# A gated expert network and a second network in one kernel: passes taken in sets, turned by block transposes and an exchange through DRAM

## The chip, the cores and the metric

The kernel runs on one core of one Trainium2 chip. The metric is the device time of one execution in microseconds; less is better. An engine here is TensorE (PE, and PEld for its weight loads), VectorE (DVE), ScalarE (ACT), GpSimd (POOL) or SyncE (SP, which only issues transfers).

## The reference, cut to what matters

```python
x = x + tanh(g_xattn) * experts(layernorm(x), token_ids, ctx)   # four experts, one for each token
x = x + tanh(g_ffn) * ffn(layernorm(x), w1, w3, w2, wr)

def experts(h, ids, W):            # Wg = Wu = Wd = ctx: one 512x512 matrix for each expert
    e = min(ids // 6250, 3)
    z = h @ W[e].T
    return (silu(z) * z) @ W[e].T

def ffn(h, w1, w3, w2, wr):        # 2048 tokens, width 512
    gates, idx = top_2(softmax(h @ wr.T))
    v = silu(silu(h @ w1.T) @ w3.T) @ w2.T
    out = zeros_like(h)
    out[idx[:, k]] += gates[:, k] * v    # only rows 0 to 7 are ever added to
```

There are 4 x 512 tokens of width 512, all in fp32. Only the first 8 rows of the output get anything from the second network, but every token contributes to them, so the second network runs over all tokens and is summed over them. The order in which it takes the tokens does not matter.

## The kernel before, in words

The kernel first sorts the tokens by expert. That gives 17 passes of 128 tokens each: 13 whole passes with one expert (0 to 12, `NF` is 13) and four split passes (13 to 16) in which each quarter of 32 tokens has its own expert. A short prelude on VectorE works out which token stands where (`from_row`, `to_row`) and which expert each pass has (`which`); TensorE runs filler matmuls (`busy`) meanwhile.

One pass goes through these steps, each a function of its own:

- `gather` (L389, POOL) fetches the pass's rows of x by an indirect DMA. `load` (L443, SP) fetches the expert's matrix, 1 MB, four for a split pass; a register load on SP finds the expert. The pool `mp` holds seven matrices.
- `centre` (L340 to L401, VectorE) takes the moments and subtracts the mean. `scale` and `norms` run `inverse_roots`, nine tiny VectorE instructions.
- `turn_in` (L380, TensorE; copy L410, ScalarE) turns the 128x512 tile by four 128x128 transposes through the identity, into PSUM (`tp_a`), and copies it to SBUF (`hT`).
- `up` (L453) multiplies by the matrix into `z`; ScalarE (L466) and VectorE (L467) form g = silu(z) z.
- `turn_mid` turns g in the same way (`tp_g`), `down` (L453) multiplies into `y`, VectorE (L481) adds to x, and POOL scatters the rows to the output (L482).
- `norms` normalizes the sum for the second network (L505), `turn_out` turns it (`tp_f`) and ScalarE copies it into `hT2`.

`z`, `y` and the second network's `v` and `Z` take turns in two PSUM buffers (`ps_mm`). A product of a whole pass is four fp32 matmuls of 128x512, each of which the profile shows as two.

The order of the work is written out by hand. `order` mixes split passes among the whole ones, and a loop runs over it: up of pass i, turn_in of i + 1, centre of i + 2, gather and load of i + 3, down of i - 1, turn_out of i - 2, and then `turn_mid` of i. So each matrix is loaded as its pass comes up, and each turn's copy lies beside a product.

The second network is a generator that `step` advances between those pieces. It takes two blocks of 1024 tokens (`b`). For each, `logits` (L699) gives the routing, `sums_of_hT` (L598 to L602) and `sums_of_w1` form the sums for a product with seven instead of eight parts (`X`, `Y`, `Z`, L622; `s1` holds the result), `route` picks the top two experts, and `second_layer` (L730 `v`, L742 `acc`) multiplies by w3 and sums over tokens. The end (`accT`, `out_product`, `ob`) finishes rows 0 to 7.

Of the kernel before, what the change touches and what calls it, by code (L numbers as in the profile page):

```python
# [17 lines left out]
ACT = mybir.EngineType.Activation  # L18

# [6 lines left out]
def tile_gated_moe_ffn(  # L26
# [58 lines left out]
    mp = ctx.enter_context(tc.tile_pool(name="mp", bufs=7))  # L85
    xp = ctx.enter_context(tc.tile_pool(name="xp", bufs=5))
    work = ctx.enter_context(tc.tile_pool(name="work", bufs=3))
    small = ctx.enter_context(tc.tile_pool(name="small", bufs=4))
    ps_mm = ctx.enter_context(tc.tile_pool(name="ps_mm", bufs=2, space=bass.MemoryType.PSUM))
# [23 lines left out]
    def load_w(src, name):  # L113
        w = ct_([P, KC, src.shape[1]], F32, name)
        nc.sync.dma_start(w, src.rearrange("(k p) f -> p k f", p=P))
        return w
# [25 lines left out]
    nc.vector.memset(steps, float(D))  # L142
    nc.vector.memset(steps[:, E - 1 : E], float(-(E - 1) * D))
# [100 lines left out]
    with nc.allow_low_precision("whole numbers below 4096"):  # L244
        nc.vector.tensor_reduce(which0, start, AX.X, ALU.add)
    nc.vector.tensor_mul(place, place, hot)
    padded = ct_([P, NJ], I16, "padded")
    with nc.allow_low_precision("whole numbers below 4096"):
        nc.vector.tensor_reduce(padded, place.rearrange("p e j -> p j e"), AX.X, ALU.add)
# [49 lines left out]
    with nc.allow_low_precision("whole numbers below 4096"):  # L299
        nc.vector.tensor_reduce(which, stepped.rearrange("p e n -> p n e"), AX.X, ALU.add)  # L300
# [4 lines left out]
    def row_tables():  # L305
# [18 lines left out]
            first, psum, float(-(NB - 1) * TB), float(TB), ALU.add, ALU.min  # L324
# [3 lines left out]
    hT2 = [ct_([P, KC, TB + (Q if b == NB - 1 else 0)], F32, f"hT2_{b}") for b in range(NB)]  # L328
# [9 lines left out]
    def moments(xt, name):  # L338
        st = small.tile([P, 6], F32, tag="st", name=f"st_{name}")
        nc.vector.bn_stats(st, xt)  # L340
        mv = small.tile([P, 2], F32, tag="mv", name=f"mv_{name}")
        nc.vector.bn_aggr(mv, st)
        return mv

    def inverse_roots(mvs_, names):
# [4 lines left out]
        def new(tag):  # L350
            return [small.tile([P, 1], F32, tag=tag, name=f"{tag}_{name}") for name in names]

        v, r, q, w, rs = new("v"), new("r"), new("q"), new("w"), new("rs")
        for i in n:
            nc.vector.tensor_scalar_add(v[i], mvs_[i][:, 1:2], EPS)
        for i in n:
            nc.vector.tensor_scalar(
                r[i].bitcast(I32), v[i].bitcast(I32), -0.5, float(0x5F3759DF), ALU.mult, ALU.add
            )
        for i in n:  # L360
            nc.vector.scalar_tensor_tensor(q[i], r[i], v[i], r[i], ALU.mult, ALU.mult)
        for i in n:
            nc.vector.tensor_scalar(w[i], q[i], 0.375, -1.25, ALU.mult, ALU.add)
        for i in n:
            nc.vector.tensor_scalar(w[i], w[i], q[i], 1.875, ALU.mult, ALU.add)
        for i in n:
            nc.vector.tensor_mul(r[i], r[i], w[i])
        for i in n:
            nc.vector.scalar_tensor_tensor(q[i], r[i], v[i], r[i], ALU.mult, ALU.mult)
        for i in n:  # L370
            nc.vector.tensor_scalar(q[i], q[i], -0.5, 1.5, ALU.mult, ALU.add)
# [11 lines left out]
    order = [0, 1, 2, 3, 4, 5, NF, 6, 7, 8, NF + 1, 9, 10, NF + 2, 11, 12, NF + 3]  # L383
    assert sorted(order) == list(range(NP))
    xs, x1s, mvs, rss, hs, hTs, gTs, gs, hs2, mats = {}, {}, {}, {}, {}, {}, {}, {}, {}, {}

    def gather(p):
        xt = xp.tile([P, D], F32, tag="x", name=f"x_{p}")
# [8 lines left out]
    def centre(p):  # L397

        mvs[p] = moments(xs[p], f"a{p}")
        hs[p] = work.tile([P, D], F32, tag="h", bufs=4, name=f"h_a{p}")  # L400
        nc.vector.tensor_scalar(hs[p], xs[p], mvs[p][:, 0:1], None, ALU.subtract)  # L401

    def scale(*ps):
        for p, rs in zip(ps, inverse_roots([mvs.pop(p) for p in ps], [f"a{p}" for p in ps])):
            rss[p] = rs

    def turn_in(p):
        tp = transposed(hs.pop(p), f"a{p}")
        hTs[p] = work.tile([P, KC * P], F32, tag="hT", bufs=2, name=f"hT_{p}")
        nc.scalar.copy(hTs[p], tp)  # L410

    def first_in(p):
# [5 lines left out]
        hTs[p] = work.tile([P, KC * P], F32, tag="hT", bufs=2, name=f"hT_{p}")  # L418
        n = D // 2
        for i in range(2):  # L420
# [7 lines left out]
            nc.scalar.copy(hTs[p][:, i * n : (i + 1) * n], tp)  # L428

    def load(p):  # L430

        n0, n = (p, 1) if p < NF else (NF + (p - NF) * G, G)
        mats[p] = []
        for i in range(n0, n0 + n):
# [4 lines left out]
                max_val=(E - 1) * D,  # L439
                skip_runtime_bounds_check_because="an expert's number, times D",  # L440
            )
            m = mp.tile([P, KC, D], F32, tag="m", name=f"m_{i}")
            nc.sync.dma_start(m, ctxT[bass.ds(at, D), :].rearrange("(k p) f -> p k f", p=P))  # L443
            mats[p].append(m)

    def expert_product(out_ps, lhs, p, inside=None):

        n = P // len(mats[p])
        for k in range(KC):
            if k == KC - 1 and inside is not None:  # L450
                inside()
            for i, m in enumerate(mats[p]):
                nc.tensor.matmul(  # L453
                    out_ps[i * n : (i + 1) * n, :],
                    lhs[:, k * P + i * n : k * P + (i + 1) * n],
                    m[:, k, :],
# [4 lines left out]
    def up(p, inside=None):  # L461
        z = ps_mm.tile([P, D], F32, tag="mm", name=f"z_{p}")
# [7 lines left out]
    def turn_mid(p):  # L470
# [3 lines left out]
        gTs[p] = gT  # L474

    def down(p):
        y = ps_mm.tile([P, D], F32, tag="mm", name=f"y_{p}")
        expert_product(y, gTs.pop(p), p)
# [12 lines left out]

    def norms(p_in, p_out):


        if p_out is None:
            return
        xt = x1s.pop(p_out)
        mv = [moments(xt, f"f{p_out}")]
        names = [f"f{p_out}"]
        if p_in is not None:  # L500
            mv.append(mvs.pop(p_in))
            names.append(f"a{p_in}")
        rs = inverse_roots(mv, names)
        h = work.tile([P, D], F32, tag="h", bufs=4, name=f"h_f{p_out}")
        nc.vector.tensor_scalar(h, xt, mv[0][:, 0:1], rs[0], ALU.subtract, ALU.mult)  # L505
# [4 lines left out]
    def turn_out(p):  # L510

        tp = transposed(hs2.pop(p), f"f{p}").rearrange("p (k t) -> p k t", k=KC)
        if p < NF:
            b, t = divmod(p, TB // P)
            nc.scalar.copy(hT2[b][:, :, t * P : (t + 1) * P], tp)  # L515
            return
        for i in range(G):
            n = (p - NF) * G + i
            place = NF * P + n * Q - (NB - 1) * TB
# [3 lines left out]
                min_val=min(place - E * (Q - 1), TB),  # L523
                max_val=min(place, TB),
                skip_runtime_bounds_check_because="its place less at most E (Q - 1) pads, at most TB",
            )
            nc.scalar.copy(hT2[NB - 1][:, :, bass.ds(at, Q)], tp[:, :, i * Q : (i + 1) * Q])

    def route(b, lt):
# [31 lines left out]
        nc.vector.tensor_sub(d, m1, m2)  # L561
        half = st("half", (P, TT))
# [10 lines left out]
        return g  # L573

    def sums_of_w1():

# [3 lines left out]
        ss = [ffp.tile([P, 2, h], F32, tag=f"S{i}", name=f"S{i}") for i in range(1, 5)]  # L580
# [10 lines left out]
    def sums_of_hT(b):  # L591


        lgs = [logits(b, half) for half in range(2)]
        b11, b12 = hT2[b][:, 0:2, 0:HB], hT2[b][:, 0:2, HB:TB]
        b21, b22 = hT2[b][:, 2:4, 0:HB], hT2[b][:, 2:4, HB:TB]
        ts = [ffp.tile([P, 2, HB], F32, tag=f"T{i}", name=f"T{i}_{b}") for i in range(1, 5)]
        nc.vector.tensor_sub(ts[0], b12, b11)  # L598
        lts[b] = [turned(b, half, lg) for half, lg in enumerate(lgs)]
        nc.vector.tensor_sub(ts[1], b22, ts[0])  # L600
        nc.vector.tensor_sub(ts[2], b22, b12)
        nc.vector.tensor_sub(ts[3], b21, ts[1])  # L602
        return b11, b21, b22, ts

    def first_layer(b):
# [14 lines left out]
        def product(out_ps, a, bb, c, start):  # L620
            for k in range(2):
                nc.tensor.matmul(  # L622
                    out_ps,
                    a[:, k, c * P : (c + 1) * P],
                    bb[:, k, :],
# [66 lines left out]
    def logits(b, half):  # L692
# [3 lines left out]
        for k in range(KC):  # L696
            cols = hT2[b][:, k, half * HB : (half + 1) * HB].rearrange("p (t c) -> p t c", t=TT)
# [14 lines left out]

    def ffn(b):

        yield from first_layer(b)
        for half in range(2):
            yield from second_layer(2 * b + half, route(2 * b + half, lts[b][half]))
# [3 lines left out]
    def second_layer(b, g):  # L721
# [3 lines left out]
        def gated(t, half=None):  # L725
# [3 lines left out]
            for k in range(KC):  # L729
                nc.tensor.matmul(  # L730
# [93 lines left out]
    SHORT = 1  # L824
    last = {b: max(i for i, p in enumerate(order) if min(p // (TB // P), NB - 1) == b) for b in range(NB)}
    running, hT_sums, lts, w1_sums = [], {}, {}, []

    def step():
        if running:
# [3 lines left out]
            if r in (0, SHORT):  # L833
                step()
# [3 lines left out]
    ffp = ctx.enter_context(tc.tile_pool(name="ffp", bufs=1))  # L838
    held = ct_([P, NU], I32, "held")

    def look_up(i):
        return which0[0:1, :] if i == order[0] else held[0:1, i : i + 1]

    load(order[0])
    gather(order[0])
    one = slice(order[1], order[1] + 1)
    nc.gpsimd.tensor_copy(held[0:1, one], which[0:1, one])
    load(order[1])  # L850
    for i in range(1, 5):
        gather(order[i])
    rest = slice(order[1] + 1, NU)
    nc.gpsimd.tensor_copy(held[0:1, rest], which[0:1, rest])
    first_in(order[0])
    scale(order[0])
    centre(order[1])
    scale(order[1])
    load(order[2])
    nc.sync.dma_start(gates[:, 0:1], g_xattn.to_broadcast([P, 1]))  # L860
    nc.sync.dma_start(gates[:, 1:2], g_ffn.to_broadcast([P, 1]))
    load(order[3])
    up(order[0], inside=lambda: turn_in(order[1]))
    centre(order[2])
    scale(order[2])
    up(order[1], inside=lambda: turn_mid(order[0]))
    turn_in(order[2])
    centre(order[3])
    nc.scalar.activation(tg, gates, AF.Tanh)
    down(order[0])  # L870
    turn_mid(order[1])
    norms(order[3], order[0])
    load(order[4])
    summing = sums_of_w1()
    owed = []
    for i in range(2, NP + 2):
        if i < NP:
            up(order[i])
        if i + 1 < NP:
            turn_in(order[i + 1])  # L880
        if i + 2 < NP:
            centre(order[i + 2])
        if i + 3 < NP:
            gather(order[i + 3])
            load(order[i + 3])
        if i <= NP:
            down(order[i - 1])
        turn_out(order[i - 2])
        if i <= NP:
            norms(order[i + 2] if i + 2 < NP else None, order[i - 1])  # L890
        step()
        if i > NP:
            step()
        if 5 <= i < 9:
# [68 lines left out]
```

## Time and profile before

| | |
|---|---|
| median of 3 runs | 277.63 us (277.48 to 277.67) |
| profiled execution | 277.53 us, its span 275.8 us |
| busy share of the span | PE 97%, PEld 45%, DVE 54%, ACT 25%, POOL 14% |
| moved by DMA | 42.54 MB; HBM read 38.10, written 4.47 |
| groups of products, busy | z 61.8, y 61.4, v 57.3 us |
| groups of turns, busy | tp_f 10.4, tp_g 10.2, tp_a 9.8 us |

A busy matmul in the profile overlaps the next one, so its mean duration (595 ns for 128x512) is longer than the distance between two. The chain of waits, followed back from the last instruction, gives each piece the time that it adds; that is the view to sum from. A group's row gives the line, engine, operation, tiles (out<-in), their shapes and the count, then the busy time and the mean of one in ns, then the idle time before it and what ended that. A line starting with a time gives start, length and what ran.

### The profile page before, as it was taken

How to read it: one execution, taken by the hardware profiler on the slowest of the kernel's cores; microseconds unless marked ns; L12 is line 12 of the kernel's file. 1: busy time of each engine (PE TensorE's matmuls, PEld its weight loads, DVE VectorE, ACT ScalarE, POOL GpSimd, SP SyncE). 2: the span in 40 equal slices, each digit the busy share in tenths (PEclk: the TensorE clock that was granted, in tenths of full speed). 3: DMA queues.
4: the chain of work that ended last, by engine and by line, in shares of the span. 5: the costliest groups of instructions: out<-in, count | busy, mean ns of one | idle time of the engine just before them, and what ended most of it. 6: DMA issues, size and time to landing. Idle time of an engine off the chain costs nothing.

```text
span 275.8 us, 3562 instructions
## 1 busy us (share of the span) xinstructions
PE 266.6 (97%) x1173; PEld 125.4 (45%) x1173; DVE 148.7 (54%) x593; ACT 69.3 (25%) x134; POOL 39.3 (14%) x63
## 2 busy tenths in 40 slices
PE   5889999999999999999999999999999999999994
PEld 2445455544355454444344444534245444344362
DVE  6677877777888769918263481516253620711000
ACT  2022232232232231223143232312113233311120
POOL 6520122221122211211110010101010000000000
PEclk9999999999999999999999999999999999999999
DMA  0697998545669996697304084001000000000000
GB/s 1 217 354 277 408 402 334 173 155 206 228 225 402 389 409 258 173 398 264 112 26 166 2 312 180 38 0 40 0 12 2 0 0 1 0 0 2 0 0 2
DMA packets 20722, 42.54 MB, mean 154 GB/s; under 512 B 2143, under 2 KB 2207, under 8 KB 20704
## 3 DMA queue, kind: packets, MB, share of 16 engines
q1 hardware_dynamic: 17952, 33.66, 34.0%
q0 software_dynamic: 2720, 8.65, 8.3%
q8 instruction: 9, 0.15, 0.2%
q14 instruction: 9, 0.07, 0.1%
q10 hardware_dynamic: 32, 0.01, 0.0%
HBM read 38.10 MB, written 4.47 MB: 154 GB/s over the span
## 4 chain that ended last, share of the span: by engine, by line
PE 94%; DVE 2%; DMA 2%; issue 1%; ACT 0%; DVEq 0%
PE z L453 22%; PE y L453 21%; PE v L730 20%; PE X L622 10%; PE Y L622 5%; PE tp_f L380 3%; PE tp_a L380 3%; PE tp_g L380 3%; PE Z L622 2%; PE acc L742 1%; PE lg L699 1%; DMA x<-in_x_dram,from_row 1%; DMA idt<-in_ids_dram 1%; PE accT L758 1%; PE o L814 0%
## 5 line engine op out<-in xcount | busy, mean ns | idle before, releaser
L453 PE MATMUL z<-m,hT 128*32 128x512 f32 (+1 forms) x232 | 61.8, 595 | 0.2 <-ACT hT L428 0.2
L453 PE MATMUL y<-m,gT 128*32 128x512 f32 (+1 forms) x232 | 61.4, 594 | 0.0
L730 PE MATMUL v<-w,s 128*128 128x512 f32 (+1 forms) x136 | 57.3, 570 | 0.0
L730 PEld LDWEIGHTS v<-w,s 128*128 128x128 f32 x136 | 25.0, 190 | 27.2 <-issue 26.7
L453 PEld LDWEIGHTS z<-m,hT 128*32 128x32 f32 (+1 forms) x232 | 22.6, 146 | 29.5 <-issue 28.1
L453 PEld LDWEIGHTS y<-m,gT 128*32 128x32 f32 (+1 forms) x232 | 22.6, 146 | 27.8 <-issue 27.8
L482 POOL DMA_INDIRECT out_dram<-x,to_row x17 | 17.2, 1011 | 84.9 <-DVE x L481 82.7
L389 POOL DMA_INDIRECT x<-in_x_dram,from_row x17 | 16.7, 984 | 77.5 <-DVE h_a L401 22.9
L467 DVE SCALAR_TENSOR_TENSOR g<-z,rs_a,g 128x512 f32<-128x512 f32 x17 | 12.7, 750 | 27.1 <-ACT g L466 27.0
L466 ACT ACTIVATE g<-z,rs_a 128x512 f32<-128x512 f32 x17 | 11.7, 687 | 51.3 <-PE z L453 51.3
L481 DVE SCALAR_TENSOR_TENSOR x<-y,tg,x 128x512 f32<-128x512 f32 x17 | 12.7, 749 | 16.9 <-PE y L453 16.8
L738 ACT ACTIVATE s<-v 128x512 f32<-128x512 f32 (+1 forms) x17 | 9.7, 572 | 41.9 <-PE v L730 41.9
L515 ACT COPY hT<-tp_f 128x512 f32<-128x512 f32 x13 | 7.6, 587 | 43.5 <-PE tp_f L380 43.5
L340 DVE BATCH_NORM_STATS2 st_a<-x 128x6 f32<-128x512 f32 x16 | 11.0, 688 | 7.5 <-DMA x<-in_x_dram,from_row 7.5
L622 PE MATMUL X<-T,S 128*128 128x512 f32 x32 | 15.0, 592 | 0.0
L380 PEld LDWEIGHTS tp_f<-ident,h_f 128*128 128x128 f32 x68 | 8.2, 141 | 10.2 <-issue 10.2
L340 DVE BATCH_NORM_STATS2 st_f<-x 128x6 f32<-128x512 f32 x17 | 11.8, 695 | 0.6
L380 PEld LDWEIGHTS tp_a<-ident,h_a 128*128 128x128 f32 x64 | 7.7, 140 | 9.4 <-issue 9.1
L640 DVE TENSOR_TENSOR s<-X,c 128x512 f32<-128x512 f32 x4 | 2.8, 692 | 16.2 <-PE X L622 16.2
L473 ACT COPY gT<-tp_g 128x512 f32<-128x512 f32 x17 | 10.0, 586 | 5.3 <-PE tp_g L380 5.3
L380 PE MATMUL tp_f<-ident,h_f 128*128 128x128 f32 x68 | 10.4, 276 | 0.0
L380 PE MATMUL tp_g<-ident,g 128*128 128x128 f32 x68 | 10.2, 273 | 0.0
(165 smaller groups left out, 271.6 us busy)
## 6 DMA issues: line engine op xcount, KB each, us to landing
m<-in_ctxT_dram SPq DMA_DIRECT2D x29, 1024.0 KB
w<-in_w1T_dram SPq DMA_DIRECT2D x1, 1024.0 KB
w<-in_w3T_dram SPq DMA_DIRECT2D x1, 1024.0 KB
w<-in_w2T_dram SPq DMA_DIRECT2D x1, 1024.0 KB
x<-in_x_dram,from_row POOLq DMA_INDIRECT x17, 6.2
out_dram<-x,to_row POOLq DMA_INDIRECT x17, 6.1
wr<-in_wrT_dram SPq DMA_DIRECT2D x1, 64.0 KB
x_first<-out_dram SPq DMA_DIRECT2D x4, 4.0 KB
```

The costliest lines, as they stand in the source:

```text
L340: nc.vector.bn_stats(st, xt)
L380: nc.tensor.transpose(tp[:, k * P : (k + 1) * P], h[:, k * P : (k + 1) * P], ident)
L389: nc.gpsimd.indirect_dma_start(out=xt, out_offset=None, in_=x, in_offset=bass.IndirectOffsetOnAxis(ap=from_row[:, p : p + 1], axis=0),)
L453: nc.tensor.matmul(out_ps[i * n : (i + 1) * n, :], lhs[:, k * P + i * n : k * P + (i + 1) * n], m[:, k, :], start=(k == 0), stop=(k == KC ...
L466: nc.scalar.activation(g, z, AF.Silu, scale=rs)
L467: nc.vector.scalar_tensor_tensor(g, z, rs, g, ALU.mult, ALU.mult)
L473: nc.scalar.copy(gT, tp)
L481: nc.vector.scalar_tensor_tensor(xt, y, tg[:, 0:1], xt, ALU.mult, ALU.add)
L482: nc.gpsimd.indirect_dma_start(out=out, out_offset=bass.IndirectOffsetOnAxis(ap=to_row[:, p : p + 1], axis=0), in_=xt, in_offset=None, bou ...
L622: nc.tensor.matmul(out_ps, a[:, k, c * P : (c + 1) * P], bb[:, k, :], start=start and k == 0, stop=k == 1, skip_group_check=True,)
L730: nc.tensor.matmul(v, s1[:, k, c_b + t * P : c_b + (t + 1) * P], w3[:, k, c0 : c0 + n], start=(k == 0), stop=(k == KC - 1),)
L738: nc.scalar.activation(s2, v, AF.Silu)
```

## The change

Four things are changed together.

First, the matrices of the four experts stay in SBUF (`cts`), loaded once by `load_cts` after the loads of passes 0, 1 and 2. From pass 3 on, `find` reads the expert's offset into a register of TensorE and the matmul's moving operand is addressed by it. Of the split passes, 13 and 15 load into `mp` (now four buffers) and 14 and 16 over `cts`.

Second, passes 4 to 11 are taken in sets. All of their up products are done before their down products. Their tiles are not turned by TensorE: VectorE's block transpose turns 32x32 blocks into a pair's buffer (inside `s1`, two passes interleaved, so the elements of one pass stand 8 apart), and `exchange` moves the blocks between partitions, four writes to DRAM and one read back, all on SP. The same is done for g, and, in sets of four passes, for the normalized sums of passes 0 to 11 (`turn_f`, `exchange_f`, three sets).

Third, `centre`'s subtraction and the normalization of passes 0 to 11 are done by ScalarE (`AF.Identity` with bias and scale), and the inverse roots of several passes by one batch.

Fourth, the order is written out anew. Pass 12 comes among the first whole passes, the split passes come last, and the second network's first block begins after pass 13. `far` holds the rows of passes 4 to 11, and later the sums T.

```diff
-    mp = ctx.enter_context(tc.tile_pool(name="mp", bufs=7))
+    mp = ctx.enter_context(tc.tile_pool(name="mp", bufs=4))
...
+    cts = ct_([P, E * KC * D], F32, "cts")
+
+    def load_cts(e):
+        nc.sync.dma_start(
+            cts[:, e * KC * D : (e + 1) * KC * D].rearrange("p (k f) -> p k f", k=KC),
+            ctxT[e * D : (e + 1) * D, :].rearrange("(k p) f -> p k f", p=P),
+        )
...
-        nc.vector.tensor_scalar(hs[p], xs[p], mvs[p][:, 0:1], None, ALU.subtract)
...
+        nc.scalar.activation(hs[p], xs[p], AF.Identity, bias=mvs[p][:, 0:1], scale=-1.0)
...
+            if p < NF or (p - NF) % 2 == 0:
+                m = mp.tile([P, KC, D], F32, tag="m", name=f"m_{i}")
+            else:
+                j = (i - n0) * KC * D
+                m = cts[:, j : j + KC * D].rearrange("p (k d) -> p k d", k=KC)
...
+    def find(p):
+
+        at = nc.values_load(
+            which[0:1, p : p + 1],
+            engines=[PE],
...
+        mats[p] = [lambda k: cts[:, bass.ds(at + k * D, D)]]
...
     def up(p, inside=None):
+        if 3 <= p < NF:
+            find(p)
...
+    def exchange(flat, name):
+
+        copy = dram.tile([P, 4, flat.shape[2]], F32, tag=name, name=name)
+        for q in range(4):
+            nc.sync.dma_start(
+                copy[q * Q : (q + 1) * Q].rearrange("f g c -> g f c"), flat[:, q, :]
+            )
+        nc.sync.dma_start(flat, copy)
...
+    pairs = {
+        j: s1.rearrange("p k t -> p (k t)")[:, (j - 2) * KC * 2 * P : (j - 1) * KC * 2 * P]
+        .rearrange("p (g t i k) -> p g t i k", g=4, i=2, k=KC)
+        for j in range(2, NS // 2)
+    }
+
+    def pair_part(p, h):
+        j, i = divmod(p, 2)
+        nc.vector.transpose(
+            pairs[j].rearrange("p q t i k -> p k q t i")[:, :, :, :, i],
+            h.rearrange("p (k q t) -> p k q t", k=KC, q=4),
+        )
...
+    def pair_columns(p):
+        j, i = divmod(p, 2)
+        part = pairs[j].rearrange("p g t i k -> p i k (g t)")[:, i]
+        return lambda k, c0, c1: part[:, k, c0:c1]
...
+    def norm_f(p):
+        rs, shift = scaled.pop(p)
+        h = work.tile([P, D], F32, tag="h", bufs=4, name=f"h_f{p}")
+        nc.scalar.activation(h, x1s.pop(p), AF.Identity, bias=shift, scale=rs)
+        hs2[p] = h
+
+    def turn_f(p):
+        b, i = divmod(p, 4)
+        nc.vector.transpose(
+            hT2[b].rearrange("p q k (i t) -> p k q i t", i=4)[:, :, :, i, :],
+            hs2.pop(p).rearrange("p (k q t) -> p k q t", k=KC, q=4),
+        )
...
+    load(2)
     nc.sync.dma_start(gates[:, 0:1], g_xattn.to_broadcast([P, 1]))
     nc.sync.dma_start(gates[:, 1:2], g_ffn.to_broadcast([P, 1]))
...
+    gather(4)
+    gather(5)
+    nc.gpsimd.memset(cts[0:1, 0:1], 0.0)
+    for e in range(E):
+        load_cts(e)
+    gather(6)
+    gather(7)
+    gather(12)
...
+    centre(12)
+    up(3)
+    scale(12)
+    down(2, inside=lambda: (turn_mid(3), turn_in(12)))
+    centre(8)
+    up(12)
+    turn_a(8)
+    centre(9)
+    down(3)
+    turn_a(9)
+    exchange_pair(4, "a")
+    scale_some(4, 4)
+    up(4, inside=lambda: turn_mid(12))
+    centre(10)
+    turn_g(4)
+    turn_a(10)
+    centre(11)
+    down(12)
+    turn_a(11)
+    exchange_pair(5, "a")
+    up(5)
+    turn_g(5)
+    exchange_pair(2, "g")
+    stats_f(0)
+    stats_f(1)
+    up(6)
...
+    exchange_pair(5, "g")
+    load(NF, 2, 4)
+    exchange_f(0)
+    for p in range(4, 8):
+        down(p)
+        stats_f(p)
+        next(summing)
...
+    roots_f(1)
+    down(8)
+    norms_turned(4, 4)
+    exchange_f(1)
+    stats_f(8)
+    down(9)
+    stats_f(9)
+    turn_in(NF)
+    centre(NF + 1)
+    down(10)
+    stats_f(10)
+    up(NF)
+    down(11, inside=lambda: turn_mid(NF))
+    load(NF + 1)
+    stats_f(11)
+    roots_f(2)
+    norm_f(8)
+    norm_f(9)
+    down(NF)
+    sums = sums_of_hT(0)
+    next(sums)
+    next(sums)
+    running.append(ffn(0))
+    norms(NF + 1, NF)
...
+    for p in range(8, 12):
+        turn_f(p)
+    exchange_f(2)
+    load_w(w3T, w3)
```

`turn_a(p)` and `turn_g(p)` are `pair_part` of the centred rows and of g, and `exchange_pair(j, ...)` is `exchange` of pair j, that is passes 2j and 2j + 1. `stats_f` takes the moments of a sum, `roots_f(b)` the inverse roots of four passes, `scale_some` those of several inputs. `sums_of_hT` is now a generator: logits of one half, logits of the other half with the first two sums T, and then one more sum at each step.

## The prediction

> **What bounds the kernel now.** I read the chain of waits first, then the same chain in order of time, the groups by shape, and the DMA rate in 2 us windows. The chain's shares by engine and line, and eight of its pieces:
>
> ```profile
> PE 94%; DVE 2%; DMA 2%; issue 1%; ACT 0%; DVEq 0%
> PE z L453 22%; PE y L453 21%; PE v L730 20%; PE X L622 10%; PE Y L622 5%; PE tp_f L380 3%; PE tp_a L380 3%; PE tp_g L380 3%; PE Z L622 2%; PE acc L742 1%; PE lg L699 1%; DMA x<-in_x_dram,from_row 1%; DMA idt<-in_ids_dram 1%; PE accT L758 1%; PE o L814 0%
> ```
> ```profile
> 27.89 3.44 PE z L453 x8
> 31.32 0.44 PE tp_a L380 x4
> 31.76 3.44 PE y L453 x8
> 35.20 0.44 PE tp_f L380 x4
> 35.63 0.44 PE tp_g L380 x4
> 36.07 3.43 PE z L453 x8
> ```
>
> Each piece starts where the one before ends: from the first z at 15.44 us TensorE is never waiting. So the time is the sum of TensorE's pieces: 3.44 us for a whole product, 0.44 us for one turn (four transposes through the identity). Whatever leaves TensorE is gained, as long as nothing else becomes late. The other engines have room on the mean, VectorE 54% and ScalarE 25% of the span; the DMA engines have none at 26 to 40 us:
>
> ```profile
> 22.00:24.00 2.00, 2.00 (x12) 1.35 (x11) 1.76 (x9) 0.97 (x2) 0.00 (x0) 1.00 0.40 133
> 28.00:30.00 2.00, 2.00 (x6) 0.88 (x5) 1.90 (x10) 0.51 (x1) 1.02 (x1) 1.00 1.05 409
> ```
>
> The last two columns are the DMA share and GB/s: 409 GB/s is the ceiling. The dip at 22 to 24 is the two loads of `gates`, 128 elements of 4 bytes each, third in the queue's order behind three matrices.
>
> Four rows price what the trace does not show directly (a strided read on VectorE, a block transpose, a strided and a plain weight load), and one answer shows the register loads:
>
> ```profile
> L300 DVE TENSOR_REDUCE which<-stepped 128x29 int32<-128x203 f32 x1 | 0.5, 525 | 0.0
> L710 DVE STREAM_TRANSPOSE lt<-lg 128x128 f32<-128x128 f32 x4 | 1.1, 303 | 2.2 <-PE lg L699 2.2
> L276 PEld LDWEIGHTS <-atlane 128*128 128x128 f16 x16 | 1.0, 152 | 1.2 <-DVE atlane L258 0.8 <-issue 0.5
> L200 PEld LDWEIGHTS <-ones 128*128 128x128 bf16 x31 | 3.3, 112 | 4.3 <-issue 1.9
> ```
> ```profile
> L520 ACTq TENSOR_LOAD <-first x16: 274/276/477, 81.8 to 208.8; - x16
> ```
>
> **What the Trainium skill says.** VectorE: DVE Perf Modes, "The three transpose paths": VectorE turns 32x32 blocks only, so blocks must still change partitions; that is what the DRAM exchange is for. `lt` in the trace is used in exactly such blocks. DMA: Bandwidth & Descriptors, "Two DMAs through the same engine are not ordered": a DMA that reads what another wrote must be issued after the first one's completion; so each exchange is two legs in series, with SP held between them. Before has no such pair. SBUF — State Buffer, "Door 1: The DMA port swizzle": steps of more than four fp32 pay per access. The trace agrees for VectorE reads and weight loads (below). No run here shows a strided write.
>
> **The change, part by part.**
>
> *Turns off TensorE.* Passes 4 to 11 lose tp_a and tp_g, passes 0 to 11 lose tp_f: 8 + 8 + 12 = 28 turns x 0.44 = **-12.3 us**. Products, logits and the second network keep their TensorE instructions. The weight loads from exchanged pairs step 8 elements. Strided against plain costs 152 against 112 ns for 16-bit; the same ratio puts the 190 ns of fp32 at 260, and a matmul lasts 430. Cost 0 behind the matmul before; without that cover, 128 loads x the excess over 430.
>
> *VectorE and ScalarE.* Sixteen `centre` (486 ns) and twelve norm (542 ns) passes leave VectorE for ScalarE, at about 0.65 us each (629 for a ScalarE SBUF pass, L647), and ScalarE loses 28 copies of 0.59: +18.2 - 16.5, nothing. VectorE gets 28 block transposes. From 303 ns for 128 elements over a floor of 155 (the one-element rows), 512 cost about 0.75 us. The 16 of inputs and g write with a step of 8; the strided reduce above costs (525 - 155) / 203 = 1.8 ns an element, so 155 + 512 x 1.8 = 1.08 us. Bounds 0.75 and 2.2; I take 1.1 for these, 0.75 for the 12 of f, whose runs are 32 long. The walk from up(4) to up(11), 31.4 us on TensorE: 8 g (0.75), 8 turn_g (1.1), 4 x 0.87 stats_f, bn of 10 and 11 1.7, turn_a 2.2, y12 0.75, two batches of roots 5.0, 4 turn_f 3.0: 31 us. VectorE is full there. Pass 12's norms then hold y of pass 4 until about 92, where its product ends at 87.6; its PSUM buffer is wanted by down(6) at 91.2: 1.5 us late, and 1.0 later at up(13). At 0.75 a transpose nothing is late. Taken: **+1.3** (0 to 2.5).
>
> *The four resident matrices.* up(3) waits for all of them. In the chain it would start at 35.9 (36.07, less a tp_f, plus a late gT copy on ScalarE behind two `centre`, +0.25). By 14 us the windows add up to 1.56 MB moved. Still to come: the rest of seven matrices at 1.05 MB, nine gathers at 0.26, one scatter and half of two more gathers: 10.35 - 1.56 = 8.8 MB at 409 GB/s = 21.5 us, plus about 2 for the `gates` dip (windows 18 to 26 lack 1.15 MB, some of which gathers can fill), plus 0.5 to land: 38.0 to 38.3. **+2.4** (0 to 5): the matrices that trickled in one per pass are now due at once. Their issue waits for a memset on POOL behind gathers 4 and 5 (1.26 us apart), at about 17; exchange a2, w1 and all later loads stand behind them on SP, none wanted before 52.
>
> *Register loads on TensorE.* Nine `find`, each a load and register arithmetic. On ScalarE's queue a load took 276 ns and, behind a waiting copy, ran only when that copy started; the copies then follow each other 0.43 apart instead of 0.27. If TensorE's sequencer runs ahead it costs 0, if not 0.3 each: **+0.9** (0 to 2.7).
>
> *Exchanges.* Eleven on SP, four of a, four of g, three of f: 14.7 MB more, against 6 MB of matrices less. Price of a leg, from the idt load (1.74 us for next to nothing): 1.7 + bytes / 409 GB/s; so 3.0 for a pair, 4.3 for f. a2: issued behind the matrices, back at 45, wanted by up(4) at 52.7. g: the last is issued at 88 and back by 97, wanted by down(10) at 106. f1 is the tight one: down(7) ends at 98.3 to 100, then stats, roots (2.5), norms and four transposes to 108 to 110, two legs 8.6: back at 117 to 119, wanted by the second logits at 121 to 123. Behind it on SP wait the loads of pass 14 (they wait for down(11) anyway, at 117; 10.2 us of data, landed 131; wanted 133.9). Cost **0**; cover 2 to 7 us. The price from the other side, the 6.1 us median of a gather of 0.26 MB, gives a leg of 8.1 and is a rival below. Scatters and gathers on POOL keep their number; the last ones only free buffers.
>
> *Order at the ends.* X after the logits waits for T and `lt` on VectorE (L598 1.22 + 0.3 after y's 0.75): **+0.55**. The last lg now comes 1.4 us after tp_f and waits for a Silu and four copies on ScalarE, 2.5: **+1.1**, before it lay 10 us later. Two late copies, at up(12) and the second y: **+0.2**; the late gT: **+0.25**.
>
> Sum: -12.3 + 1.3 + 2.4 + 0.9 + 0 + 0.55 + 1.1 + 0.45 = **-5.6 us**. The profiled execution took 277.53 (span 275.8 and 1.7 around it), 0.1 from the median of the runs; so **271.9**. A measurement here tells 0.2% (0.55 us) from no change.
>
> **Rivals.**
>
> *Everything hides*: transposes at 0.75, matrices in time, registers free. 277.5 - 12.3 + 1.1 + 0.55 = 266.3, at the very best 265.2. For it: each stall has zero within its bounds. Against: the strided read's 1.8 ns, and 409 GB/s is a hard ceiling.
>
> *Late transfers*: a leg costs 8.1 us for 1 MB. f1 is back at 126 where 122.8 is wanted, +3.4: 275.3. For it: 6.1 us for a quarter MB. Against: that is from POOL, with its descriptor work of 1 us and a busy queue.
>
> *Slower: VectorE becomes the bound.* Ten strided transposes lie between up(4) and down(4). From 1.1 us on each further 0.1 us is 1.0 us of lag, and TensorE follows two PSUM buffers behind. It decides from 1.65 us a transpose, where the 5.6 are eaten; at 2.2, the upper bound, 271.9 + 11 = 283. For it: no strided write is in the trace. Against: strided reads cost 1.75 times, not 3 times.
>
> *The change does not do what it says*: the split passes still load 16 matrices, so DMA only falls from 29 to 23; if the matrices were what bounds, little would change. The chain says they do not.
>
> **The numbers.** Forecast 0.56 (269 to 275), everything hides 0.22, late transfers 0.11, VectorE-bound 0.11. 271.9 is the likeliest. Range 265.5 to 279: the forecast, nearly all of the first rival, the second, and the mildest of the third. Faster: 0.55 + 0.22 + 0.08 = 0.85; same 0.03; slower 0.12.
>
> **What would show it.** Right: no tp of passes 4 to 11, tp_a, tp_g and tp_f groups of 32, 36 and 20 transposes; z waiting for DMA once, 2 to 3 us, near 36; strided transposes near 1.1 us; VectorE over nine tenths at 53 to 90; weight loads under 300 ns. Wrong: X or lg waiting for DMA near 120; weight loads above 430; a gap of 0.3 us at each find; z waiting for exchanged pairs. A total under 266 would mean that the stalls hide, over 277.5 that one of the last two rivals holds.

## The result, and the profile after

The changed kernel takes **334.06 us** (median of 4 runs, 332.51 to 335.16) where the kernel before, on the same chip, takes 277.62 (277.48 to 277.67): a ratio of 1.203, 95% interval 1.198 to 1.208. The forecast was 271.9, at most 279.0. It was wrong in sign and by 62 us. Where the executions of one kernel below fall into two groups some per cent apart, its time and ratio are those of the faster group; only the profile of the kernel with one load behind each of four exchanges is of the slower one.

The page of the profile after: the span, the busy time of TensorE, and three of the rows of 40 slices (8.3 us each).

```profile
span 330.7 us, 3331 instructions
...
PE 273.9 (83%) x1061; PEld 132.6 (40%) x1061; DVE 144.4 (44%) x464; ACT 74.0 (22%) x134; POOL 38.9 (12%) x64
...
PE   5999379999979409788106999959999999999995
PEclk9999869999979957979656999999999999999999
DMA  0889953643347663844439627997400000000000
```

TensorE, which never waited before from its first product on, now has holes at slices 5, 14 and 15, 20 to 22 and 27. The clock row falls to 5 to 7 at and behind most of them. At 5 and 27 the DMA row shows 9, loads that fill the engines; in the longest hole, 20 and 21, it shows 4 and 3: there the DMA engines are far from full. The waits say for what (engine, line, what was waited for, us in total, times, longest):

```profile
PE lg L843 <- DMA hT<-f: 19.5, 2, 16.5
PE y L514 <- DMA s<-g: 15.1, 2, 12.7
PE z L514 <- DMA cts<-in_ctxT_dram: 7.1, 1, 7.1
PE z L514 <- DMA m<-in_ctxT_dram: 6.8, 4, 1.8
```

35 us of waits are for what exchanges brought back (`hT<-f`, `s<-g`), 7.1 for the resident matrices at up(3), 6.8 for loads of split passes. The chain, which was 94% TensorE before, can be followed back to 188 us only; the second fence is a piece of it in order of time:

```profile
PE 35%; DMA 5%; ACTq 1%; ACT 1%; issue 0%; DVE 0%
```
```profile
202.24 2.45 PE X L766 x6
204.69 14.90 DMA m<-in_ctxT_dram
```

Those loads of pass 15 could not be issued before 201.7, when SP was done with f2. SP's own waits and its instructions between 132 and 172 us show what held it (start, length, queue, line, what, how many):

```profile
SPq L567 <- DMA f<-hT: 37.7, 7, 9.1
SPq L567 <- DMA g<-s: 29.1, 8, 7.2
SPq L567 <- DMA a<-s: 28.6, 6, 9.2
```
```profile
132.19 8.46 SPq L564 DMA_DIRECT2D f<-hT  x4
153.02 0.35 SPq L567 DMA_DIRECT2D hT<-f  x1
153.47 2.92 SPq L564 DMA_DIRECT2D f<-hT  x4
171.03 0.35 SPq L567 DMA_DIRECT2D hT<-f  x1
```

L564 is the write leg, L567 the read leg. f1's write begins at 153.47 and is read at 171.03: 17.6 us for a leg that I had at 4.3. f0's, behind two loads of matrices, took 20.8. The first 5 us of f1's write go beside f0's read of 1 MB, with a DMA share of 0.70 to 0.97 from 155 to 158 us; then the engines empty. No engine computes from 162 to 176; the windows within f1's write there give the DMA share and GB/s in the last two columns:

```profile
166.00:167.00 1.00, 0.00 (x0) 0.00 (x0) 0.00 (x0) 0.00 (x0) 0.00 (x0) 0.50 0.25 96
168.00:169.00 1.00, 0.00 (x0) 0.00 (x0) 0.00 (x0) 0.00 (x0) 0.00 (x0) 0.50 0.26 100
```

A share of 0.25 at 100 GB/s fits four of sixteen engines busy all the time. The target of each write is `copy[...].rearrange("f g c -> g f c")`: its outermost dimension is the four groups g. The Trainium skill, DMA: Bandwidth & Descriptors, "Why a DMA increments its semaphore by 16 and not by 1", says under "How many engines (k)" that a DMA takes "the largest k ≤ 16 that divides both of those dim sizes", the slowest dimensions of its two sides. I had read the page for another of its sections. That is the theory that the experiments test first; the rivals are that short runs or DRAM writes are slow in themselves, and that SP's order does the harm.

### The profile page after: what moved, and what is told of

Its sections match the earlier page's. It is cut to its first block, busy times and chain, and to the rows that moved or that the text cites. A ratio compares the mean times of both kernels' runs of the same rounds, so it can differ in the third digit from the quotient of the medians.

```text
span 330.7 us, 3331 instructions
## 1 busy us (share of the span) xinstructions
PE 273.9 (83%) x1061; PEld 132.6 (40%) x1061; DVE 144.4 (44%) x464; ACT 74.0 (22%) x134; POOL 38.9 (12%) x64
## 5 line engine op out<-in xcount | busy, mean ns | idle before, releaser
L514 PE MATMUL y<-cts,s 128*128 x64 | 33.6, 675 | 15.2 <-DMA s<-g 15.1
L514 PEld LDWEIGHTS y<-cts,s 128*128 128x128 f32 x64 | 19.7, 319 | 27.4 <-issue 19.6
L514 PE MATMUL z<-m,hT 128*32 128x512 f32 (+1 forms) x88 | 24.6, 668 | 7.0 <-DMA m<-in_ctxT_dram 6.8
L514 PE MATMUL z<-cts,s 128*128 x64 | 28.5, 598 | 0.1
L514 PEld LDWEIGHTS z<-cts,s 128*128 128x128 f32 x64 | 19.9, 314 | 8.0 <-DVE g L530 1.0
L514 PE MATMUL z<-cts,hT 128*32 128x512 f32 (+1 forms) x80 | 16.2, 618 | 7.1 <-DMA cts<-in_ctxT_dram 7.1
L529 ACT ACTIVATE g<-z,rs_a 128x512 f32<-128x512 f32 x17 | 11.7, 686 | 46.1 <-PE z L514 42.0
L514 PE MATMUL y<-m,gT 128*32 128x512 f32 (+1 forms) x88 | 18.3, 596 | 0.0
L766 PE MATMUL X<-far,S 128*128 128x512 f32 x32 | 15.1, 595 | 0.6 <-ACT u L777 0.6
L514 PEld LDWEIGHTS z<-m,hT 128*32 128x32 f32 (+1 forms) x88 | 6.9, 143 | 21.6 <-DMA m<-in_ctxT_dram 10.9
L544 DVE SCALAR_TENSOR_TENSOR far<-y,tg,far 128x512 f32<-128x512 f32 x8 | 6.0, 745 | 21.5 <-PE y L514 21.5
L766 PE MATMUL Y<-far,w 128*128 128x512 f32 x32 | 15.2, 592 | 0.0
```

The lines of the kernel that those rows point to most:

```text
L514: nc.tensor.matmul(out_ps[i * n : (i + 1) * n, :], lhs(k, i * n, (i + 1) * n), m(k), start=(k == 0), stop=(k == KC - 1),)
L529: nc.scalar.activation(g, z, AF.Silu, scale=rs)
L544: nc.vector.scalar_tensor_tensor(xt, y, tg[:, 0:1], xt, ALU.mult, ALU.add)
L766: nc.tensor.matmul(out_ps, a[:, k, c * P : (c + 1) * P], bb[:, k], start=start and k == 0, stop=k == 1, skip_group_check=True,)
```

## The experiments

Ratios are to the kernel before, run beside it on the same chip, with 95% intervals. Exchanges are named by what they carry and by pair or set: a4 is the a of passes 8 and 9, f1 the f of passes 4 to 7.

### Writes by source group

```
-        for q in range(4):
-            nc.sync.dma_start(copy[q * Q : (q + 1) * Q].rearrange("f g c -> g f c"), flat[:, q, :])
+        for g in range(4):
+            nc.sync.dma_start(
+                copy[:, g, :].rearrange("(q f) c -> f q c", q=4), flat[g * Q : (g + 1) * Q])
         nc.sync.dma_start(flat, copy)
```

> The same bytes go to the same places in the same runs of 1 and 2 KB by four DMAs, but each DMA now takes the 32 partitions of one source group (outermost dimension 32 on both sides) instead of all 128 partitions with the target's four groups outermost. Theory (the outermost 4 confines each write to 4 of the 16 DMA engines): DMA share during writes rises from 0.26 towards 1, the SP wait between write and read falls from 7 to 9 us to 2 to 3, logits and down products wait for exchanges 0 to 3 us in all instead of 35, and the whole lands at 268 to 276 us, 272 the likeliest. Rival (short runs or DRAM writes themselves are slow, about 100 GB/s): no change, 330 to 336 us. Second rival (SP in order is what hurts, with loads behind exchanges): legs hardly shorter, total above 310 us.

289.07 us, ratio 1.036 (1.029 to 1.042); span 287.7 against 330.7. Four lines and the same bytes gave back **43 us** of span. f1's write now leads to its read in 8.9 us instead of 17.6, the pair a3 in 5.5 instead of 9.1. But the time is 13 us above the upper end of this run's forecast. Two waits of size stay; the forecast had given 0 to 3 us to all waits for exchanges:

```profile
123.25 2.55 SPq L564 DMA_DIRECT2D f<-hT  x4
132.14 0.34 SPq L567 DMA_DIRECT2D hT<-f  x1
```
```profile
PE lg L843 <- DMA hT<-f: 7.0, 1, 7.0
PE z L514 <- DMA cts<-in_ctxT_dram: 4.5, 1, 4.5
```

### The permutation in the read leg

```
-        for g in range(4): ...
-        nc.sync.dma_start(flat, copy)
+        nc.sync.dma_start(copy, flat)
+        for q in range(4):
+            nc.sync.dma_start(
+                flat[q * Q : (q + 1) * Q], copy[:, q, :].rearrange("(g f) c -> f g c", g=4))
```

> One plain write of 128 partitions with runs of 4 or 8 KB, then four reads, each into 32 partitions, in runs of 1 or 2 KB: the permutation is made by the read leg, and all five DMAs have an outermost dimension of 32 or 128. Theory (number of engines): as fast as the version that writes by source group, within 2 us of it, 268 to 276 us. Rival (short runs into DRAM are slow, reads are not): clearly faster than the version that writes short runs, by 20 us or more, since here only the read has short runs.

294.07 us, 1.053 (1.046 to 1.059): 40 us better than the change as well, though 5 us behind the version before it, not within 2. Long runs into DRAM are no better than short ones: that rival falls. Here one DMA writes a pair, and where nothing stands ahead (a4, a5) its write leads to the reads in 3.1 and 3.0 us, which is the price that the prediction had. Why the whole is 5 us slower was not followed up; it waits 8.9 us for f1 and 2.7 for a pair of g.

### Two engines

```
         for q in range(4):
+            for g in (0, 2):
                 nc.sync.dma_start(
-                    copy[q * Q : (q + 1) * Q].rearrange("f g c -> g f c"), flat[:, q, :])
+                    copy[q * Q : (q + 1) * Q, g : g + 2].rearrange("f g c -> g f c"),
+                    flat[g * Q : (g + 2) * Q, q, :])
```

> The changed kernel with each write cut in two, so that the outermost dimension of each of the eight DMAs is 2 instead of 4; same bytes, same runs, same places. Theory (the outermost dimension sets the number of DMA engines): the DMA share during an f write falls from 0.26 to 0.13 and the rate from about 100 to about 50 GB/s, a pair's write takes 11 to 14 us, and the total is 370 to 420 us. Rival (the order of rows or the short runs set the rate): the rate stays at 80 to 100 GB/s and the total within 330 to 350 us, the four more issues of 0.5 us each included.

404.99 us (one run). Windows during f1's write, which now takes 25.6 us up to its read:

```profile
218.00:222.00 4.00, 0.00 (x0) 0.00 (x0) 0.00 (x0) 0.00 (x0) 0.00 (x0) 0.50 0.13 51
```

Outermost dimension 4: share 0.25, 100 GB/s. Outermost dimension 2: share 0.13, 51 GB/s. Half the share, half the rate: some 25 GB/s for each of four or two engines, and 409 / 16 is 25.6. So runs of 1 and 2 KB cost no rate here. This settles it between the two readings: with the same bytes, runs and places, the rate follows the outermost dimension. (A pair took 14.4 to 14.9 us where 11 to 14 were forecast.)

### Order alone, with the narrow writes

The changed kernel with an own matrix for pass 3 and early loads of pass 13 (both edits are shown below), and its own writes.

> The changed kernel with its writes confined as they were (outermost dimension 4), but with the two repairs of order: an own matrix for pass 3 and the early loads of pass 13. If order on SP was the main fault, this alone comes near the version with both, under 285 us. If the four engines of the writes are the main fault, the legs stay at 7 to 9 us for a pair and 13 or more for f, SP is still occupied by them, and the total stays above 300 us; 312 is my estimate.

336.38 us (one run), no better than the change at all, and 24 above the estimate for it. These two changes of order gain nothing while the writes are narrow; they are not what made the 43 us.

### No exchange

```
     def exchange(flat, name):
+        return
```

> Leaves out all eleven exchanges, writes and reads, so products and logits of passes 0 to 11 read blocks that have not changed partitions; every other instruction stays. Theory (the exchanges alone make the loss): 267 to 273 us, the sum of my prediction without them, with up(3) waiting 2 to 4 us for the resident matrices and no other wait of TensorE above 1.5 us. Rival (resident matrices, the register loads or VectorE make a large part): above 280 us, with waits of TensorE for those. The difference to the kernel with wide writes is what eleven exchanges cost when they use all DMA engines; I expect 0 to 4 us.

278.35 us, ratio 0.995 (0.993 to 0.998); span 276.9. The theory had said 267 to 273, so at least 5 us of loss lie outside the exchanges. And eleven exchanges on all engines cost 10.8 us of span (287.7 - 276.9), where 0 to 4 were forecast. Apart from the start (2.9 us, in every kernel here), the waits have one entry of size:

```profile
PE z L514 <- DMA cts<-in_ctxT_dram: 5.6, 1, 5.6
```

The product behind it took 5.59 us instead of 3.4 to 3.7, in a stretch (35 to 50 us) with a mean clock of 0.77: 7.6 us in all at a place where I had put 2.4.

### An own matrix for pass 3

On the version that writes by source group:

```
     nc.sync.dma_start(gates[:, 1:2], g_ffn.to_broadcast([P, 1]))
+    load(3)
...
-        if 3 <= p < NF:
+        if 4 <= p < NF:
             find(p)
```

> On the version that writes by source group: pass 3 loads its own matrix into the fourth buffer ahead of the four resident ones, which are then first wanted by up(12), about 10 us later. Theory (up(3) stands 4.5 us for the resident matrices, and its product then runs 1.9 us longer at half the granted clock): that wait goes to under 0.5 us, up(12) does not wait, and about 6 us go: 281 to 284 us. Rival (the DMA engines are full there in any case, so one more MB only moves the wait): up(12) waits 3 to 6 us instead and the total stays at 287 to 290.

283.58 us, 1.021 (1.014 to 1.027), as the theory had it; span 280.8, so 6.9 us less. The resident matrices are first wanted by up(12) now, which waits 0.7 us and not the rival's 3 to 6. The logits still wait for f1:

```profile
46.06 3.67 PE L514 MATMUL z<-cts,hT 128*128 x8 [0.69 <-DMA cts<-in_ctxT_dram]
...
130.15 1.93 PE L843 MATMUL lg<-hT,wr 128*32 128x128 f32 x32 [4.76 <-DMA hT<-f]
```

### Both stalls taken away

The kernel of the last experiment with `return` in `exchange`.

> Leaves out all eleven exchanges, as the earlier kernel without them did, and has the own matrix for pass 3: the changed kernel without either of its two stalls. Theory (the other terms of my sum hold: -12.3 for the turns, +1.3, +0.9, +0.55, +1.1, +0.45 for VectorE, register loads and the order at the ends, and 1 us for strided weight loads that I had at nothing): 269 to 272 us, 2 to 3% faster than before. Rival (VectorE, the register loads or the strided loads cost more than I had them at): 274 us or more, with waits of TensorE that name them.

270.99 us, 0.976 (0.974 to 0.979); span 269.1, as forecast.

```profile
PE X L761 <- DVE lt L849: 1.1, 1, 1.1
PE z L514 <- DMA cts<-in_ctxT_dram: 1.0, 1, 1.0
```

So everything but exchanges and the resident stall is, in total, as the sum had it, within 1.3 us. Between this kernel and the one with mended exchanges lie 11.7 us of span, and the next five runs move the four loads of pass 13 about to find them.

### Five places for four loads

In the change, two of these loads stand ahead of the write of g4 and two ahead of f0's; each is 1 MB. f0's write then waits for them, and f1's write, whose data was ready at 114 us in the version with mended writes, was issued there at 123, behind f0's. All five kernels stand on the one with an own matrix for pass 3, and their loads take the place of its `load(NF, 0, 2)` and `load(NF, 2, 4)`.

```
# all four on SP behind a4
     exchange_pair(4, "a")
+    load(NF)
# one each on SP behind a4, a5, g2, g3
+    load(NF, 0, 1)
...
# on ScalarE's queue: two behind a4 and two behind a5 in the program, started at 53 and 62 us
+    load(NF, 0, 2, ACT)
...
# on ScalarE's queue: two behind g3 and two behind g5 in the program, started at 71 and 85 us
# on ScalarE's queue: two behind a5 and two ahead of g3 in the program, started at 65 and 74 us
```

> On the kernel with an own matrix for pass 3: the four loads of pass 13 are issued together after exchange a4, at about 65 us, when their buffers are free and the DMA engines carry about 170 GB/s, instead of two at 86 and two at 107 ahead of the writes of g4 and f0. Theory (f1 is late because SP issues in order: g4 and f0 are written behind 2 MB of loads each, and f1's write waits 9 us on SP behind f0): f1 is back by 122 to 126 us, the 7.0 us wait of the logits and the half clock behind it go, the 1.5 us wait of z goes too: 270 to 276 us, faster than before. Rival (f1 is late by its own length): the logits still wait 4 us or more and the total stays above 278.

> On the kernel with writes by source group and an own matrix for pass 3: the four loads of pass 13 are issued one at a time, each behind the read of one exchange (a4, a5, g2, g3), at 63 to 84 us, so that no exchange stands behind more than 1 MB of them. Theory (the early loads in one block only moved the wait: a5's write stood on SP's queue and on the DMA engines behind 4 MB, 14 us; f1 was back in time): no product waits for an exchanged pair more than 1 us, f1 is back by 118 to 124 us, the 4.8 us wait of the logits, the 1.3 us of half clock behind it and the 1.1 us wait of z go: 273 to 277 us, between 0.5 and 2% faster than before. Rival (the DMA engines have no room for 17 MB of exchanges beside the matrices, in whatever order): the waits move on to other pairs, and the total stays at 281 or more.

> On the kernel with writes by source group and an own matrix for pass 3: the four loads of pass 13 are issued from ScalarE's DMA queue, two at about 64 us and two at about 70, so that no exchange stands behind them in SP's queue[...]. Theory (an exchange is late when a load stands ahead of it in the same queue, and SP then holds every later exchange): a pair's exchange takes 6 to 8 us throughout, f1 is back by 118 to 123 us, the waits of logits (4.8) and z (1.1) and the half clock behind them go: 273 to 277 us. Rival (what the DMA engines carry in all is the limit between 60 and 110 us): the loads slow the exchanges as much as before, products wait for pairs 4 us or more, 281 us or more.

> As the version before, with the loads on ScalarE's queue, but later: all four at about 79 to 87 us. Theory: g4's exchange shares the engines with the loads and takes 8 to 10 us instead of 9, g5 and f0 no longer stand behind 2 MB each, f0's write is read by 107 instead of 115.6, f1 is back by 121 to 124: the waits of logits and z go: 273 to 277 us. Rival (the engines' total is the limit): g4 or g5 is late by 3 us or more and the total stays at 281 or more.

> As the two versions before, with the loads of pass 13 on ScalarE's queue two and two, at about 63 us (behind the write of a5) and about 72 us (behind that of g2). In the early version the first two went out at 53 us and a4's write was held on SP until one of them had landed (7.4 us); in the late one g2 took 12 us. Theory (each late exchange is one that has a load ahead of it at its own moment of need; there is room between): a4 read by 64 us, a5 by 72, g2 by 79, f1 back by 121: no wait of TensorE for an exchanged pair or f above 1 us, 271 to 275 us, 1 to 2.5% faster than before. Rival (whatever the place, one exchange of the SP chain ends up late): 277 us or more.

None reached what was expected. In the order of the edits: 284.89 us, 1.020 (1.014 to 1.027); 284.28, 1.024 (1.020 to 1.027); 278.53, 1.002 (0.999 to 1.004); 281.77, 1.015 (1.011 to 1.020); 280.28, 1.010 (1.007 to 1.013). (The 17 MB of exchanges in the second expectation are 14.7, as in the prediction.) Against the 1.021 that they start from, the two places on SP's queue gain nothing. On ScalarE's queue the third gains nearly 2% and the last about 1%, though none is faster than the kernel before. The first, the third and the last in their waits:

```profile
PE z L514 <- DMA s<-a: 9.4, 1, 9.4
```
```profile
PE z L514 <- DMA s<-a: 4.5, 1, 4.5
```
```profile
PE z L514 <- DMA s<-a: 4.4, 1, 4.4
```

The logits wait no longer in these three, f1 is back; instead an up product waits for the pair whose exchange got the loads ahead of it: a5, a4, a5. In the third the loads were on another queue, and still SP held a4's write for 7.4 us until one of them had landed; why is not shown. In the fourth, which has no such line, the logits still wait 2.1 us. In the last, up(12), which lies ahead of the moved loads, waited 1.9 us for the resident matrices and its product took 5.37 us instead of 3.67, so about 3 us of its loss are not due to the place. In these three places moving the loads moved the wait, at a smaller price on ScalarE's queue. That left two readings: no order found yet, or too much traffic.

### The g exchanges taken back

```
     def turn_g(p):
-        pair_part(p, gs.pop(p))
+        j, i = divmod(p, 2)
+        tp = transposed(gs.pop(p), f"g{p}")
+        nc.scalar.copy(
+            pairs[j].rearrange("p g t i k -> p i k (g t)")[:, i],
+            tp.rearrange("p (k c) -> p k c", k=KC))
         gTs[p] = pair_columns(p)
...
-    up(5)
-    turn_g(5)
-    exchange_pair(2, "g")
+    up(5, inside=lambda: turn_g(4))
```

and so on up to `down(4, inside=lambda: turn_g(11))`. The first kernel issues the loads of pass 13 on SP behind a5, the second leaves them where the change has them in the program.

> On the kernel with writes by source group and an own matrix for pass 3: the eight turns of g go back to TensorE (four transposes each inside the next up product, ScalarE copies them into the layout of the pairs), the four g exchanges are gone, and the loads of pass 13 are issued together behind exchange a5. Theory (what is left of the loss is the traffic between 50 and 120 us: 8 pairs at 1 MB, f0 and f1 at 2 MB and 5 MB of loads on one SP queue; 4 MB and four in-order waits less leave room): no wait of TensorE for a pair or f above 1 us, 8 x 0.44 = 3.5 us more on TensorE than the 269.1 us span without exchanges, 1 to 2 us of waits: span 273 to 275, 275 to 277 us, just faster than before (0.3 to 1%). Rival (order alone, some wait whatever the amount): up products wait 4 us or more for a5, or logits for f1, 280 us or more.

> The same with the loads of pass 13 where the change had them (two behind up(7), two ahead of f0). Theory of the amount: with the g exchanges gone nothing but f0 stands behind them, f0 is read by 112 us and f1 is back by 123: no logits wait above 1 us, 275 to 277 us, like its sister. Theory of the order: f0's write stands behind 2 MB as before and f1 behind f0; logits wait 3 to 5 us, 279 to 282 us.

**276.13 us, 0.988 (0.986 to 0.990)**, and 275.84 us, 0.990 (0.987 to 0.993). Both came in as forecast and are faster than the change and, by 1%, than the kernel before. The first in its longest waits, all of them small and none for an exchange:

```profile
PE cnt L202 <- DVE hot L199: 3.0, 1, 3.0
PE z L514 <- issue: 1.7, 2, 1.5
PE tp_a L463 <- DVE h_a L458: 0.9, 1, 0.9
```

The pair does not compare two places: without g exchanges the second kernel's loads have nothing to hold them, and SP issues them at 70 us, against 69 in the first. What it shows is that four exchanges less, 4.2 MB and four waits on SP, leave room. Whether the bytes or the waits counted, and whether all eleven exchanges would fit in some other order, stays open.

## Why the prediction was wrong, step by step

The spans add up: 330.7 (change) - 43.0 (writes on all engines) = 287.7; - 6.9 (own matrix for pass 3) = 280.8; - 11.7 (no exchange at all) = 269.1, which is 6.7 under before. These are single executions on several chips, on which the kernel before took 277.6 to 279.2 us; taken from the ratios, the steps are about 46, 4 and 12 us.

*Exchanges, "cost 0".* This is the step that failed, at the term bytes / 409 GB/s. The ceiling was measured on loads that spread over 16 engines, and I applied it to a write on which only four work. From write to read it is 8.9 to 9.4 us for five of the eight pairs instead of 3.0, and 17.6 for f1 instead of 4.3. On all engines it is 4.4 to 5.5 for those five and 8.9 for f1. Of what is left above the price, part is the issue of four writes one after another, some 1.9 us on SP, where the price has one start: as one DMA, a pair took 3.0. The second part of the term, the cover of 2 to 7 us, was reckoned for each exchange alone. They share one in-order queue: SP stood at L567 for 95 us in all, and even on 16 engines six pairs, two f and five matrices between 50 and 120 us left some exchange late (11.7 us). The rival "late transfers" had the symptom, a slow leg and a late f1, but took the cause from POOL's gathers, and had f1 as the only victim, at 3.4 us.

*The four resident matrices, +2.4 (0 to 5).* Right place, wrong size: 7.1 in the change and 5.6 without exchanges. I let the whole 8.8 MB move at 409 GB/s; from 20 to 35 us the trace of the version with mended writes has 364 with a share of 0.97. At that rate the 21.5 us become 24.2, which is an estimate and most of the difference; no run tests it alone. Nor is 409 a hard ceiling: the change moves 426 GB/s at 174 to 175 us.

*What no term had: the clock.* The Trainium skill, TensorE: Matmul & The Clock Gate, Part 1, says that an idle window of about 3.4 us halves the clock. The trace agrees: TensorE stops at 155.5 us, but for a burst of logits at 158.5 to 159.9; the clock is at 1.00 in 158 to 159, 0.57 in the next window and 0.50 from then on; it starts at 176.4 and is back at 1.00 in 180 to 181.

```profile
159.00:160.00 1.00, 0.88 (x24) 0.43 (x12) 0.00 (x0) 0.00 (x0) 0.00 (x0) 0.57 0.27 106
180.00:181.00 1.00, 1.00 (x4) 0.46 (x3) 0.93 (x6) 0.00 (x0) 0.00 (x0) 1.00 1.08 406
```

(The clock is the third column from the right.) TensorE is busy 273.9 us in the change and 257.9 with the stalls gone, for the same 1061 instructions: of the 61.6 us between the two spans **16.0 are longer running**, only 45.6 standing still. That the lower clock makes these 16.0 is read from the clock row; no run tests it alone.

*Turns, -12.3, and the small terms, +4.3.* In the kernel with both stalls gone, 269.1 against 275.8 is -6.7, where turns and small terms make -8.0. Right in sum, within 1.3, in part by luck, since the single terms miss in both directions. VectorE was busy 30.3 of 35 us at 53 to 88 and delayed no product by more than 0.2 (I had +1.3, and "over nine tenths"); the register loads took 0.3 us and showed no gap (+0.9 was too much); the last logits waited for nothing (+1.1); X after `lt` waited 1.1 (0.55), up(12) 1.0 for matrices. The transposes were priced well, the weight loads not, in these groups of the change:

```profile
L514 PEld LDWEIGHTS y<-cts,s 128*128 128x128 f32 x64 | 19.7, 319 | 27.4 <-issue 19.6 <-DVE g L530 3.2
L579 DVE STREAM_TRANSPOSE s<-g 128x512 f32<-128x512 f32 x8 | 8.9, 1107 | 0.8
L620 DVE STREAM_TRANSPOSE hT<-h_f 128x512 f32<-128x512 f32 x12 | 7.5, 673 | 0.0
```

1.1 and 0.67 us against 1.1 and 0.75; but 319 ns against 260 for a strided weight load. It hides behind the matmul nearly as expected: in the kernel with both stalls gone 56 matmuls of the up products took 24.53 us (59.45 to 83.98), 438 ns each instead of 430, so about 1 us for all 128. The rival "VectorE becomes the bound" falls with the 1.1 us.

*The chances.* 0.12 for slower was far too little. The list of what would show it named one right line, lg waiting for DMA; for pairs it named z, and in the change it was y that waited. What was missing is a bound for the unknown from above: I had no large DMA with a small outermost dimension to price from, and the gather's 6.1 us for a quarter of a MB was set aside as a case of POOL's.

*Slips that decide nothing.* The sum of "everything hides" gives 266.9 by its own terms, not 266.3. Passes 3 to 12 are ten `find`, not nine. The terms of the 10.35 MB add up to 10.2. And the trace of before does have one read that waits for a write, the load of `x_first` behind the last scatter; it was not used as a price.

## What to carry to other kernels

Before a DMA gets a price, look at the outermost dimension of both its sides: four there gave a quarter of the engines, and writing the same bytes by source group instead of target group was worth 43 us of 331. Then add up what one in-order queue has to do in a stretch, waits included; when moving a transfer only moves the wait, try taking traffic away: four exchanges less brought more than any of five new places for the loads. And count a long wait of TensorE at more than its length: behind the one that ended at 176.4 us it ran at half the clock for about 3 us.

## What the runs showed of the hardware that I had not expected

A DMA write whose outermost dimension is 4 moves 96 to 100 GB/s at a share of 0.25, with 2 it moves 51 at 0.13; that is about 25 GB/s for each engine, as in loads on all sixteen at 409. A ScalarE copy of 128x512 out of PSUM takes 1092 ns when it writes with a step of 8 elements, against 584 for a plain one, in the kernel without g exchanges:

```profile
L599 ACT COPY s<-tp_g 128x512 f32<-128x512 f32 x8 | 8.7, 1092 | 14.2 <-PE tp_g L412 14.2
...
L536 ACT COPY gT<-tp_g 128x512 f32<-128x512 f32 x9 | 5.3, 584 | 15.6 <-PE tp_g L412 15.6
```

The register loads of TensorE, 0.3 us without exchanges, have a median of 1.3 us and a longest of 1.6 in the change, without a gap in its products of passes 4 to 11.
